# A planner's dates for the pieces of the turning groups, and three expert tiles as column pieces in the last group

## The chip, the core and the metric

The kernel runs on one core of one Trainium2 chip. The metric is the device time of one launch in microseconds, the median of several runs. The core's engines are TensorE (PE, with its weight loads as PEld), VectorE (DVE), ScalarE (ACT), GpSimd (POOL) and SyncE (SP); each works through its own instructions in program order, and they wait for each other by semaphores. DMAs are issued from the queues of SP and POOL.

## What is computed

The reference is one transformer layer on x of 4 x 2048 x 512 float32: xn = layernorm(x), and then x + attention(xn) + experts(xn).

```
qkv = xn @ w_qkv                          # 16 heads of 32
q, k = spectral_filter(q), spectral_filter(k)   # linear: folded into the weights
out = softmax(q k^T / sqrt(32)) v ; out @ w_out + b_out
# top-1 experts: one shared weight, capacity 100 for each of 8 experts
best = argmax(softmax(xn @ w_gate)); rank within the expert; tokens of rank >= 100 are dropped
y[token] = gate * (xn[token] @ w_expert + b_expert)   # at most 800 tokens
```

## The kernel before, in words

The work is a loop over 16 groups, numbered k = 0 to 15: 4 batches of 4 groups of 4 heads. A group is 4 blocks of 512 queries, a block 16 halves, a half one tile of 128 keys; so a group has 64 halves (GH) and the whole loop 1024. "Half 31 of group 7" is half 7 x 64 + 31. Two halves make a window. Nearly all instructions go through the helper `InOrder`, so that the profile gives them one line, 82, and one reads by the tiles' names.

A half has on PE: the scores of 4 heads against one tile of keys (`steps_of_keys,q`), the same for the row maxima of a block 21 halves ahead (`keys,q`), and the products of the half before with the values (`even,v`, `odd,v`, each over 32 columns for each head). DVE reduces the maxima (`part`) and adds up the products (`num`), ACT takes the exponentials into the tiles `even` and `odd` (3 buffers for odd), POOL issues a DMA for each window that adds odd to even, and adds windows on its own.

Beside that, each half executes a list of further steps, `agenda[half]`, in the order in which `at(half, step, cost=...)` (line 930) filled it. Costs are in pieces. A **piece** (cost 1) is one 128 x 128 tile of the next group's queries, keys or values, made by `query_key` or `value` from 32 matmul records of 128*32 weights by 128 columns, and copied out of PSUM by ACT; there are 48 for each group. Others are the closing of the block before (`fold` of the row sums in half 5 of a block, 8 reciprocals in halves 6 to 13, then, a block later, the output `result` in halves 1 to 4, cost 1 each, and the output's DMA `add` in half 5), the loads of weights by SP, and every fourth group the stage of the next batch. The four banks of PSUM beside the scores go round by age; a half with costs reduces two maxima together where their banks are neighbours (`max_reduce`).

In the **turning groups** k = 3, 7 and 11 the next batch's tokens are normalized (ACT) and turned (4 transposes on PE, an ACT copy, cost 0.5), and then routed to the experts by 29 steps (`plan_route`: gate scores, cost 4, transposes of the logits, exponentials, ranks and 16 entries into tables).

Who places the pieces: `plan(k)` is called for every group. In most groups it files the pieces in three queues (queries, keys, values) with a release and a last half each, and `level` gives each half, up to a load, the piece with the earliest last half, and looks ahead where it would rather wait. In the turning groups `spread` takes turns and pieces in one fixed order, written out by `projections`, and spaces them evenly by cost until the group's last half.

The experts (`expert_steps`, `place_experts`) come when all tokens are routed: from half 36 of group 12 on, 7 tiles of 128 slots are gathered from x by POOL's indirect DMAs, measured and scaled. `expert(i)` works as a pipeline: tile i is normalized, tile i - 1 turned, tile i - 2 multiplied by the expert weight in 4 full matmuls of 128 x 128 by 512 (cost 4), given its bias by DVE and its gate by ACT; the products fall into halves 2, 4 to 14 of group 13. Then each tile's rows of the output are gathered (POOL, `yg`), added (POOL) and scattered back, two halves apart, one tile in each block from group 13 on (halves 26, 42, 58 of group 13, 10, 26, 42, 58 of group 14). The gathers and scatters wait for the output's earlier DMAs.

The last group projects nothing further, so many of its halves have nothing on their agenda.

Of the kernel before, what the change touches and what calls it, by code (L numbers as in the profile page):

```python
# [12 lines left out]
F32 = mybir.dt.float32  # L13
# [21 lines left out]
ST = -(-SLOTS // P)  # L35
NTAB = 4
# [7 lines left out]
CROWDED = (1, (B - 1) * NG + 2)  # L44
# [57 lines left out]
def attention_and_top1_experts(ctx: ExitStack, tc: tile.TileContext, a: dict, out: bass.AP):  # L102
# [364 lines left out]
    def projections(k, tiles=1, kinds=None):  # L467
# [3 lines left out]
        if k == 0:  # L471
            order = [(query_key, 0, 1), (query_key, 0, 0)]
            order += [(query_key, n, 1) for n in range(1, NQ)] + [(query_key, 1, 0)]
            order += [(value, n) for n in range(NQ)] + [(query_key, n, 0) for n in range(2, NQ)]
        else:
            first = 2 if k in CROWDED else 3 if k % NG == 0 else 4
            queries, vals = ([(f, n, *s) for n in range(NQ)] for f, *s in ((query_key, 0), (value,)))
            news = [(query_key, n, 1) for n in range(NQ)]
            if first == 4:
                order = vals + queries[:2] + news + queries[2:]  # L480
            else:
                order = vals[:first] + queries[:1] + news[:3]
                order += vals[first : first + 1] + news[3:] + vals[first + 1 :] + queries[1:]
# [83 lines left out]
    def expert_steps():  # L567


        def begin():  # L570
# [15 lines left out]
            for half in xg:  # L586
                on.gpsimd.memset(half, 0.0)
# [3 lines left out]
            taken.update(mv=mv, w_exp=w_exp, b_exp=b_exp, entry=entry, index=index, bound=bound, xg=xg)  # L591

# [19 lines left out]

        def expert(i):

            if i >= 2:
# [11 lines left out]
            if 1 <= i <= ST:  # L627
                px = bank()
                for r in range(NR):
                    on.tensor.transpose(px[:, r * P : (r + 1) * P], row(i - 1)[:, r * P : (r + 1) * P], ident)  # L630
                taken["xt"] = work.tile([P, QB], F32, tag="byx", name="xt", bufs=1)
                on.scalar.copy(taken["xt"], px)
            if i >= 2:
                on.scalar.activation(row(i - 2), row(i - 2), AF.Copy, scale=taken["entry"][:, at, 1])
# [6 lines left out]
        return begin, fetch, measure, scale, expert  # L641

    def gather_row(i):
        taken["sum"] = work.tile([P, DM], F32, tag="byx", name="yg", bufs=1)
# [282 lines left out]
    heads = [[] for _ in agenda]  # L927
    costs = [0.0] * len(agenda)
    ended = {}

    def at(half, step, *args, cost=0):
        agenda[half].append(lambda: step(*args))
        costs[half] += cost
# [51 lines left out]
    def spread(steps, last, latest={}):  # L985


        base = steps[0][1]

        def places(level):  # L990
            half, done, found = base, costs[base], []
            for place, (cost, first, _) in enumerate(steps):
                stop = latest.get(place, last + 1)
                while half < stop and (half < first or done + cost / 2 > level * (half - base + 1)):
                    half += 1
                    if half > last:
                        return None
                    done += costs[half]
                done += cost
                found.append(half)  # L1000
            return found

        found = next(filter(None, (places(level / 32) for level in range(16, 400))))
        for (cost, _, step), half in zip(steps, found):
            at(half, step, cost=cost)
        return found

# [11 lines left out]
    def plan_route(first, step):  # L1019
# [3 lines left out]
        for i in range(ROUTE):  # L1023
            at(first + halves[i], step, i, cost=costs_of.get(i, 0))

    def place_experts(start):


        begin, fetch, measure, scale, expert = expert_steps()
        first = start + 36  # L1030
        at(first, begin)
        for i in range(ST):
# [3 lines left out]
        for i in range(ST + 2):  # L1036
            at(first + 26 + 2 * i, expert, i, cost=(NR if i >= 2 else 0) + (1 if 1 <= i <= ST else 0))
        for i in range(ST):
            free = start + GH + i * HB + 26
# [4 lines left out]
    def plan(k):  # L1044
# [3 lines left out]

        def after_keys_are_spent():

            for i, place in enumerate([j for j, s in enumerate(kinds) if s == 1]):
                cost, _, step = steps[place]
                steps[place] = cost, start + SPENT + i // TQ * TQ, step
                latest[place] = start + SPENT + i // TQ * TQ + 3 * TQ - 1

# [6 lines left out]
        last = start + GH - 1  # L1062
        steps, kinds, latest = [], [], {}
        if k == 0:
# [7 lines left out]
            plan_route(24, lambda i: first_route[i]())  # L1072
        if c == NG - 2 and b + 1 < B:
# [13 lines left out]
        if c < NG - 1 or k >= FREE:  # L1087
            for s in range(3):
                mine = [piece for piece, kind in zip(pieces, kinds) if kind == s]
                for i, piece in enumerate(mine):  # L1090
                    n = i // TQ
                    if s == 0:
                        stop = start + GH - MAX_AHEAD // 2 - 1 + n * HB
                        release = start + 1 + n * HB
                    elif s == 1:
                        release = start + SPENT + n * TQ
                        stop = release + 3 * TQ - 2
                    else:
# [226 lines left out]
```

## Time and profile before

| what | us |
|---|---|
| median of 3 runs | 4136.39 (4134.75 to 4137.25) |
| the profiled execution | 4136.57 |
| its span, first to last instruction | 4134.8 |
| PE busy | 4114.6 |
| DVE, POOL, ACT busy | 3416.0, 3016.6, 2487.0 |

The profile is of one execution. Its span leaves out 1.77 us around the instructions. PE's granted clock is full (1.00) throughout. "Busy" for matmuls includes the time for which they are in flight, and four matmuls over 32 columns each run at once; so a share of 100% says that PE always has something in flight, not how much work a stretch holds. For that one cuts the span into stretches and compares their lengths: the profile gives, for each stretch, its length and each engine's busy time with its count of instructions.

### The profile page before, as it was taken

To read this page: it belongs to the slowest core of one execution; us is meant where nothing else is said; L and a number is where in the kernel's file an instruction comes from. 1 tells how busy PE (TensorE), PEld (TensorE's weight loads), DVE (VectorE), ACT (ScalarE), POOL (GpSimd) and SP (SyncE) were. 2 spreads that over 40 slices of the span, in tenths; PEclk is the share of its full clock that TensorE was granted. 3 is DMA by queue.
4 is the path that set the end of the run, shared out by engine and by line. 5 is a ranking of instruction groups with operands and counts; after the bars stand their busy time and mean duration, and the time that the engine had idled before them with its cause. 6 is when DMAs were issued, how large, how long until landed. Compare 5 with 4: busy or idle time off the path is not lost.

```text
span 4134.8 us, 121347 instructions
## 1 busy us (share of the span) xinstructions
PE 4114.6 (100%) x52824; PEld 1834.2 (44%) x52824; DVE 3416.0 (83%) x4890; ACT 2487.0 (60%) x3424; POOL 3016.6 (73%) x2122
## 2 busy tenths in 40 slices
PE   8999999999999999999999999999999999999999
PEld 5444444444444444444444444444444444444433
DVE  7788887977888888897788888888778887888885
ACT  4555565676665556567565556566656555666665
POOL 1678776676887777676778777767678785787877
PEclk9999999999999999999999999999999999999999
DMA  4687887987788778898777887889877886788787
GB/s 127 144 164 155 162 163 158 227 189 144 153 158 162 156 158 167 189 208 187 143 152 157 162 162 154 169 192 205 171 154 153 174 164 132 162 166 171 158 163 154
DMA packets 179486, 680.78 MB, mean 165 GB/s; under 512 B 23478, under 2 KB 54360, under 8 KB 114184
## 3 DMA queue, kind: packets, MB, share of 16 engines
q0 software_dynamic: 109856, 601.63, 74.4%
q1 hardware_dynamic: 69024, 71.34, 5.2%
q8 instruction: 414, 6.78, 0.6%
q14 instruction: 120, 0.98, 0.1%
q10 hardware_dynamic: 72, 0.03, 0.0%
HBM read 71.07 MB, written 87.91 MB: 38 GB/s over the span
## 4 chain that ended last, share of the span: by engine, by line
PE 97%; DVE 2%; issue 0%; ACT 0%; DMA 0%; SPq 0%; ACTq 0%
PE array L82 97%; DVE part L82 2%; DVE num L82 0%; DVE factor L82 0%; DMA odd<-in_L_attn_w_qkv_dram 0%; ACT xs L82 0%; ACT xnT L82 0%; ACT odd L82 0%; DVE stats L82 0%; DVE xs L82 0%; ACT w L82 0%; DVE mv L82 0%; DVE neg L82 0%; SPq L82 0%; SPq L133 0%
## 5 line engine op out<-in xcount | busy, mean ns | idle before, releaser
L82 DVE TENSOR_REDUCE part<-array 128x1 f32<-128x512 f32 (+1 forms) x3089 | 2480.2, 858 | 641.1 <-PE array L82 636.1
L82 POOL TENSOR_TENSOR even<-even 128x1024 f32<-128x1024 f32 x876 | 2125.1, 2531 | 451.1 <-DMA even<-odd 450.3
L82 PE MATMUL array<-keys,q 32*128 32x512 f32 x8192 | 2049.2, 613 | 4.3 <-ACT keys L82 0.8
L82 PE MATMUL array<-q,steps_of_keys 32*128 32x512 f32 x8128 | 2015.1, 614 | 0.1
L82 ACT ACTIVATE odd<-array 128x1024 f32<-128x1024 f32 x1024 | 995.7, 1021 | 459.4 <-PE array L82 385.6
L82 ACT ACTIVATE even<-array 128x1024 f32<-128x1024 f32 x1014 | 983.8, 1021 | 420.7 <-PE array L82 412.6
L82 PEld LDWEIGHTS array<-keys,q 32*128 32x128 f32 x8192 | 767.2, 184 | 555.4 <-DVE part L82 341.0
L82 PEld LDWEIGHTS array<-q,steps_of_keys 32*128 32x128 f32 x8128 | 691.3, 184 | 242.3 <-issue 228.8
L82 DVE TENSOR_TENSOR num<-num,array 128x512 f32<-128x512 f32 x960 | 649.1, 676 | 32.8 <-PE array L82 31.3
L82 POOL DMA_DIRECT2D even<-odd x504 | 461.5, 916 | 278.8 <-ACT odd L82 237.0
L82 PEld LDWEIGHTS array<-xnT,w 128*32 128x32 f32 x16384 | 459.6, 110 | 276.9 <-DVE part L82 188.8
L82 PE MATMUL array<-odd,v 128*32 128x512 f32 x4096 | 545.7, 605 | 0.5 <-DVE part L82 0.5
L82 PE MATMUL array<-even,v 128*32 128x512 f32 x4056 | 540.4, 605 | 0.3 <-DVE part L82 0.3
L82 PE MATMUL array<-xnT,w 128*32 128x128 f32 x16384 | 531.8, 273 | 1.5 <-ACT xnT L82 1.0
L82 PEld LDWEIGHTS array<-w,xnT 128*32 128x32 f32 x8192 | 231.1, 110 | 145.6 <-DVE part L82 102.7
L82 DVE RECIPROCAL factor<-den 128x64 f32<-128x64 f32 x504 | 273.6, 544 | 0.0
L82 PE MATMUL array<-w,xnT 128*32 128x128 f32 x8192 | 269.8, 273 | 0.2
L82 PE MATMUL array<-wo,ot 128*32 128x512 f32 x2048 | 266.1, 592 | 0.0
L82 PEld LDWEIGHTS array<-odd,v 128*32 128x32 f32 x4096 | 81.0, 108 | 388.1 <-DVE part L82 380.3
L82 PEld LDWEIGHTS array<-even,v 128*32 128x32 f32 x4056 | 80.1, 108 | 384.5 <-DVE part L82 380.0
L82 POOL DMA_DIRECT2D out_dram<-y x63 | 85.6, 1359 | 164.1 <-ACT y L82 115.3
L82 ACT COPY q<-array 128x128 f32<-128x128 f32 x256 | 67.9, 265 | 178.4 <-PE array L82 178.4
(150 smaller groups left out, 1532.8 us busy)
## 6 DMA issues: line engine op xcount, KB each, us to landing
even<-odd POOLq DMA_DIRECT2D x504, 1024.0 KB, 8.2
out_dram<-y POOLq DMA_DIRECT2D x63, 1024.0 KB, 9.6
xs<-in_L_attn_x_dram SPq DMA_DIRECT2D x96, 256.0 KB
out_dram<-in_L_attn_x_dram SPq DMA_DIRECT2D x16, 1024.0 KB
w<-wd SPq DMA_DIRECT2D x30, 256.0 KB
w<-in_L_attn_w_qkv_dram SPq DMA_DIRECT2D x16, 256.0 KB
wo<-in_L_attn_w_out_dram SPq DMA_DIRECT2D x16, 256.0 KB
negm<-row SPq DMA_DIRECT2D x192, 4.0 KB
```

Of the source, the lines that this page charges most:

```text
L82: done = act(*args, **kwargs)
```

## The change

Four edits.

1. Turning groups file their pieces in the three queues like all others; `spread` is gone, and so is the special order of `projections`. Turns stand at dates written out by hand (`TURNS`, the halves in which `spread` had put them). A piece is released one half after the turn of the tile with its number. `level` then decides.
2. Normalizing, turns and the routing steps go into `tails`, which are appended to the agenda after `level`: they stand behind the pieces of their half.
3. Expert tiles 0 to 3 stay as they are. Tiles 4, 5 and 6 are turned in halves 14, 24 and 29 of the last group, and each is multiplied in four column pieces of 128 output columns (the same 32 matmul records as a value piece), with the bias added by DVE from PSUM, in halves 15, 16, 22, 23; 25 to 28; and 30, 31, 32, 38. Their gathers, adds and scatters follow in halves 25, 27, 29; 30, 32, 34; and 39, 41, 43 of the last group, and use the keys' weight buffer for the gathered rows.
4. The second memset of the gathered rows moves from half 36 to half 41 of group 12.

```diff
+EARLY = 4
+LATE = ((14, 15, 16, 22, 23), (24, 25, 26, 27, 28), (29, 30, 31, 32, 38))
...
-            first = 2 if k in CROWDED else 3 if k % NG == 0 else 4
...
+            order = [(query_key, n, s) for s in range(2) for n in range(NQ)] + [(value, n) for n in range(NQ)]
...
+        def turn_row(i):
+            px = bank()
+            for r in range(NR):
+                on.tensor.transpose(px[:, r * P : (r + 1) * P], row(i)[:, r * P : (r + 1) * P], ident)
+            taken["xt"] = work.tile([P, QB], F32, tag="byx", name="xt", bufs=1)
+            on.scalar.copy(taken["xt"], px)
+
+        def expert_columns(i, q):
+            cols = slice(q * P, (q + 1) * P)
+            pe = bank()[:, cols]
+            for r in range(NR):
+                columns(
+                    pe,
+                    taken["xt"][:, r * P : (r + 1) * P],
+                    taken["w_exp"][:, r, cols],
+                    start=(r == 0),
+                    stop=(r == NR - 1),
+                )
+            on.vector.tensor_tensor(row(i)[:, cols], pe, taken["b_exp"][:, cols], ALU.add)
+            if q == NR - 1:
+                on.scalar.activation(row(i), row(i), AF.Copy, scale=taken["entry"][:, i : i + 1, 1])
...
         def expert(i):
-            if i >= 2:
+            if 2 <= i < EARLY + 2:
...
     def gather_row(i):
-        taken["sum"] = work.tile([P, DM], F32, tag="byx", name="yg", bufs=1)
+        if i < EARLY:
+            taken["sum"] = work.tile([P, DM], F32, tag="byx", name="yg", bufs=1)
+        else:
+            taken["sum"] = weights.tile([P, NR, P], F32, name="w1", bufs=1).rearrange("p r n -> p (r n)")
...
+    def behind(half, step, *args, cost=0):
+        tails[half].append(lambda: step(*args))
         costs[half] += cost
...
         for i in range(ROUTE):
-            at(first + halves[i], step, i, cost=costs_of.get(i, 0))
+            behind(first + halves[i], step, i, cost=costs_of.get(i, 0))
...
+        at(first + 5, clear_rest)
...
+        tail = start + 3 * GH
+        for i, (turned, *places) in enumerate(LATE):
+            at(tail + turned, turn_row, EARLY + i, cost=0.5)
+            for q, half in enumerate(places):
+                at(tail + half, expert_columns, EARLY + i, q, cost=1)
         for i in range(ST):
-            free = start + GH + i * HB + 26
+            free = start + GH + i * HB + 26 if i < EARLY else tail + (25, 30, 39)[i - EARLY]
...
+            for i in range(NT):
+                turned[i] = start + TURNS[i]
+                behind(turned[i] - 1, in_stage, 3, i)
+                behind(turned[i], in_stage, 4, i, cost=0.5)
...
+                release = max(release, turned.get(i, start - 1) + 1)
...
+    TURNS = (2, 4, 6, 6, 6, 7, 7, 8, 12, 12, 12, 13, 16, 19, 21, 22)
...
     level(0, END)
+    for steps, last_ones in zip(agenda, tails):
+        steps += last_ones
```

## The prediction, on record before the changed kernel ran

> **What bounds the kernel now.** I read the page first, then the table by stretches, cut at the start of each half's value products (scores and maxima of half h+1 thus count in half h), then the chain of waits and POOL's timeline in the last group. TensorE is the bound nearly everywhere:
>
> ```profile
> PE 4114.6 (100%) x52824; PEld 1834.2 (44%) x52824; DVE 3416.0 (83%) x4890; ACT 2487.0 (60%) x3424; POOL 3016.6 (73%) x2122
> ...
> PE 97%; DVE 2%; issue 0%; ACT 0%; DMA 0%; SPq 0%; ACTq 0%
> ```
>
> Busy time does not tell how much a half costs; its length by what the planner put into it does. Six halves of group k = 7, numbers 8, 14, 16, 28, 29 and 31; the first columns are start:end, length and PE busy with its count:
>
> ```profile
> 1895.13:1899.65 4.52, 4.52 (x63) 2.11 (x60) 3.05 (x5) 2.70 (x5) 0.00 (x0) 1.00 0.98 224
> 1920.98:1924.78 3.80, 3.80 (x60) 1.79 (x56) 3.01 (x5) 2.21 (x4) 3.80 (x3) 1.00 0.94 188
> 1928.70:1933.08 4.38, 4.38 (x64) 2.21 (x60) 3.03 (x5) 2.81 (x5) 4.09 (x2) 1.00 0.90 181
> ...
> 1981.36:1986.04 4.68, 4.68 (x93) 2.64 (x89) 3.48 (x6) 2.49 (x5) 4.62 (x5) 1.00 0.63 130
> 1986.04:1989.46 3.42, 3.32 (x28) 1.14 (x24) 3.42 (x7) 2.25 (x3) 1.91 (x2) 1.00 0.91 208
> ...
> 1992.85:1998.51 5.66, 5.66 (x128) 3.62 (x125) 2.81 (x6) 2.76 (x7) 5.02 (x5) 1.00 0.87 177
> ```
>
> A piece is 32 matmul records. So a half without a piece (x28) takes 3.4 us, with one (x60) 3.80, with two (x93) 4.67, with three (x128) 5.66: the first costs 0.4, each further one 0.87. The empty half is not PE's: DVE is busy for all of its 3.42 us. The same lengths return in every group to about 0.02 us (a half with a result instead of a piece: 3.78, with both: 4.66; the last half of a block with one piece and with two: 3.91 and 4.79). So the sum can be made half by half, once it is known where the planner puts things; I worked its rules through for both versions, and for the one before they give the count of matmuls in each half of the trace.
>
> An expert tile beside the scores is dear (group 13, halves 12 and 14, the latter without a turn):
>
> ```profile
> 3451.28:3458.69 7.41, 7.41 (x41) 3.28 (x37) 4.59 (x7) 3.25 (x5) 5.90 (x5) 1.00 0.71 143
> ...
> 3462.49:3469.04 6.55, 6.55 (x36) 2.41 (x32) 3.70 (x6) 2.42 (x4) 5.43 (x3) 1.00 0.78 159
> ```
>
> In the last group, where halves 15, 16, 22 to 32 and 38 to 41 are empty, the chain of waits shows the cycle of such a half, which runs through DVE (reductions, sum, reciprocal) and not through PE:
>
> ```profile
> 3992.32 1.27 DVE part L82 x2
> 3993.59 0.59 DVE num L82
> 3994.19 0.46 DVE factor L82
> 3994.65 0.79 DVE part L82 x2
> ```
>
> **The change, part by part**, against the profiled execution (4136.57 us; span 4134.8 and 1.77 around it; 0.18 above the median of 4136.39).
>
> *Pieces in turning groups (k = 3, 7, 11).* The planner takes a piece out of nine halves: 24 (7.23 to 6.36, the length of half 24 of group 0, which has the gate scores and no piece), 28, 42, 56, 62 (4.67 to 3.80), 31 (5.66 to 4.79), 37 and 52 (4.66 to 3.78), 47 (4.79 to 3.91): 6 x 0.87 + 3 x 0.88 = 7.86. It fills 29 (3.42), 30 (3.39) and half 0 of the next group (3.44) to 3.80: 0.38 + 0.41 + 0.36; and doubles 32: 0.87. Net -5.84, three times: **-17.5**. The pieces do not vanish. After k = 3 and 7 five more fall into groups 6 and 10: halves 13, 14, 15, 16, 20, 21 go from one load to two (3 x 0.87 + 3 x 0.88 = 5.25), half 12 from two to one (-0.87): +4.38, twice: **+8.8**. After k = 11 three land in halves that the experts leave (next part), one in half 44 of group 14 (**+0.87**), one in the last group (below).
>
> *Expert tiles out of group 13.* Halves 10 and 12 go from 7.40 to 3.80 and half 14 from 6.56 to 3.80, each with one piece; half 8 keeps a tile and loses a turn of 4 transposes (34.1 us for 224: 0.61). 3.60 + 3.60 + 2.76 + 0.61: **-10.6**.
>
> *Columns in the last group.* A column piece has the 32 matmuls and shapes of a value piece, so each half goes to the length with a piece: 15 (3.43 to 3.91), 16 (3.41), 22 (3.43), 23 (3.39), 25 (3.39), 26 (3.64), 28 (3.42), 30 (3.39), 32 (3.42), 38 (3.43) to 3.80, 27 (3.60 to 4.00), 31 (3.27 to 3.91): +4.80. Turns: half 14 from 3.80 to 4.52; half 24 gets a turn and the piece left over, 3.39 to 4.52; half 29 a turn alone, 3.39 to 3.65 (half 0 of group 13): 0.72 + 1.13 + 0.26. Together **+6.9**.
>
> *Order.* Turns and routing steps now stand behind the pieces of their half. Of the halves shown, 8 (turn, then piece) took 4.52 and 16 (piece, then turn) 4.38; 13 and 22 are like 8. Three halves in three groups: 9 x 0.14 = 1.3. Group 0 has its routing steps ahead of the pieces, the turning groups already behind; the transposes of logits (half 26 of groups 0 and 7):
>
> ```profile
> 193.38:198.47 5.09, 5.04 (x65) 2.42 (x61) 4.29 (x8) 2.26 (x4) 3.42 (x2) 1.00 0.83 169
> ...
> 1972.89:1977.37 4.48, 4.45 (x65) 2.21 (x61) 3.84 (x8) 2.21 (x4) 3.43 (x2) 1.00 0.92 187
> ```
>
> That is 0.60; half 46 (4.64 against 4.44) and half 31 (4.94 against 4.79) give 0.35. Together **-2.2**. The Trainium skill, TensorEngine Tiling (Array Packing), Tiling Modes, says that a change of tiling mode, not of tile, drains the TensorE; a turn uses the full array between column tiles, so by that rule either order has two drains and this term would be 0. The rows speak against it.
>
> *DVE's share of a column piece.* A value piece is emptied by ACT (0.27), a column piece by DVE: 128x128 from PSUM, nearest row 0.29 (placed). In seven of the twelve halves (22, 23, 25 to 28, 38) a reciprocal stands ahead of it, and DVE has about 0.33 idle in a half with a piece and a reciprocal before the next reductions (timeline around 3935): nothing, if the add fits. Against that, the 0.22 of the block's negated maximum lengthens such a half from 3.80 to 4.00, and a measurement of 0.84 one to 4.10. Bounds 0 and 7 x 0.3 = 2.1; I take the nearest size, 7 x 0.2: **+1.4**. The bank is freed later too; that is in the 0.2.
>
> *POOL.* Three gathers (1.09), adds (1.59) and scatters (1.08) move to the last group: 11.3 us. Queued behind them on POOL are the pairs' DMAs, which free the odd buffers that ACT writes. From half 39 on:
>
> ```profile
> 4050.44 0.85 POOL L82 DMA_DIRECT2D even<-odd  x1
> 4056.40 4.67 POOL L82 TENSOR_TENSOR even<-even 128x1024 f32<-128x1024 f32 x2 [5.11 <-DMA even<-odd]
> 4061.03 0.73 POOL L82 TENSOR_TENSOR xnT<-keys 64x256 f32<-64x256 f32 x1
> 4061.72 0.84 POOL L82 DMA_DIRECT2D even<-odd  x1
> ...
> 4068.49 0.88 POOL L82 DMA_DIRECT2D even<-odd  x1
> ...
> 4070.30 1.22 POOL L82 DMA_DIRECT2D even<-odd  x1
> ```
>
> Tiles 4 and 5 meet 2.19, 2.03, 1.03 and 0.72 of idle time. The last gather (half 39) waits for the output DMA of 4040.44 (median 9.6 to landing) and fits into the 5.11. The last add and scatter (halves 41, 43), 2.7, meet a POOL without idle time until 4081.7. The pair of 4068.49 then lands later by 8.2 counted from its issue, at 4076.7, and ACT's odd tile started at 4076.89. Lower bound 0 (half 38 makes PE 0.4 to 0.6 later, and POOL may catch up); upper bound 5.0 (2.7, 1.25 left over from the scatter of half 34 with its issue, and the gather's 1.09 if its wait outlasts the 5.11). PE reads that tile's banks about 1.2 after ACT is done. I take 2.7 + 1.25 - 0.6 - 1.2, about **+2.0**. The memset moved to half 41 of group 12 (2.1) goes into POOL time before tile 4's fetch and costs nothing; if it were late, that fetch has five halves. The weight loads on SP go with the last piece of their kind, as before, and come at least five halves (19 us) ahead of the next pieces of that kind: 0; were one late, the first piece of its kind would wait for what is left of it.
>
> Sum: -17.5 + 8.8 + 0.9 - 10.6 + 6.9 - 2.2 = -13.7; + 1.4 + 2.0 = -10.3: **4126.3 us**.
>
> **Rivals.**
> *Both covers hold*: DVE's adds fit the 0.33 and POOL's lag is caught up. -13.7, 4122.9. For it: POOL idles 17 us from 3985 to 4061. Chance 0.22.
> *POOL decides the end*: both bounds, 2.1 + 5.0: 4136.57 - 13.7 + 7.1 = 4130.0. For it: no idle after 4056.4. Chance 0.17.
> *Order gives nothing* (what counts is the switch, not its neighbour; by the rule named above): 4126.3 + 2.2 = 4128.5. Against it: the rows of halves 16 and 26. Chance 0.11.
> *Slower: waits for the output on POOL's queue.* Gathers and scatters wait for each other and for the output's DMAs. At full price: 11.3 of work, 9.6 before the last gather, 3.5 (median landing) ahead of each add and of the second gather, 14: 34.9. Three odd buffers cover 4 halves, 15.2, less 0.9 and 8.2: 6.1. The rest, 28.8, would stall PE: 4136.57 - 13.7 + 1.4 + 28.8 = 4153. It makes the kernel slower from 13.7 - 1.4 + 8.3 = 20.6 uncovered. Against it: between gather and add lie two halves, and POOL's idle time. Chance 0.05.
>
> **Numbers.** Forecast 0.45, own range 4124.3 to 4128.3. A measurement of this kernel tells 0.2% (8.3 us, so 4128.1) from no change. Faster: the first rival, 0.40 of the forecast and 0.03 of the third, 0.65. Same: the second, the rest of the third and 0.05 of the forecast, 0.30. Slower 0.05. Range 4122.0 to 4130.5: from the first rival, less a little, to just past the second.
>
> **What would show it.** Halves 29 and 30 of groups 3, 7, 11 at 3.80 with x60, half 31 at x93; half 13 to 16 of groups 6 and 10 at 4.67; no 7.4 in group 13 after half 8; halves 22 to 28 of the last group at 3.8 (adds fit) or 4.0; ACT odd waiting for a DMA near half 49 (POOL). Wrong, if an empty half costs more than 3.80 once it has a column piece, or if the doubled halves of groups 6 and 10 lose more than 0.87.

## The result, and the profile after

| what | us |
|---|---|
| kernel before, median of 22 runs | 4136.64 (4134.75 to 4138.56) |
| changed kernel, median of 22 runs | 4131.34 (4129.44 to 4133.74) |
| ratio | 0.9988, 95% interval 0.9982 to 0.9993 |
| profiled execution of the changed kernel, and its span | 4130.40, 4128.6 |

The change saves 5.3 us, 0.12%, where 10.3 were forecast; 4131.3 lies above the range. Between the profiled executions the difference is 6.17, of which 1.24 come from the stretch ahead of the loop, which the change does not touch; so the halves give 4.93, and these are what has to be explained. The profiled execution of the changed kernel is 0.94 below its median. One half may account for that: half 32 of group 4 takes 4.67 in it, as in the kernel before, but 5.3 to 6.3 in 15 of the 18 profiles of kernels with the turning edit (this one and those of the experiments). With the turning edit alone, PE stands still there for 1.19 us inside a piece, and the profile names nothing that it waits for.

From the page of the changed kernel, its busy times and the chain that ended last, in which DMA has 1% (0% before) and POOL now appears:

```profile
PE 4105.5 (99%) x53184; PEld 1832.0 (44%) x53184; DVE 3418.3 (83%) x4876; ACT 2486.1 (60%) x3424; POOL 3015.6 (73%) x2122
...
PE 97%; DVE 1%; DMA 1%; POOL 0%; issue 0%; ACT 0%; SPq 0%; POOLq 0%; ACTq 0%; DVEq 0%
```

PE's busy time fell by 9.1 us, the span by 6.2. So PE is idle for 2.9 us more than before, and the chain says that some of its waiting is for DMAs.

The table by stretches again, cut at the same places (start:end, length, PE busy with its count; the third column from the end is the granted clock). Half 26 of group 0; halves 8, 29 and 31 of group 7; half 13 of group 6; half 12 of group 13; halves 22 and 23 of the last group:

```profile
192.14:196.62 4.48, 4.45 (x64) 2.20 (x60) 3.84 (x8) 2.22 (x4) 3.42 (x2) 1.00 0.94 190
1890.75:1895.14 4.39, 4.39 (x64) 2.22 (x61) 3.06 (x5) 2.71 (x5) 1.75 (x2) 1.00 1.14 261
...
1979.50:1983.30 3.80, 3.80 (x60) 1.79 (x56) 3.48 (x6) 2.20 (x4) 3.21 (x2) 1.00 0.99 226
...
1987.10:1991.89 4.79, 4.79 (x97) 2.71 (x93) 3.00 (x5) 2.72 (x6) 4.44 (x4) 1.00 0.82 166
1651.95:1656.62 4.67, 4.67 (x92) 2.63 (x89) 3.48 (x6) 2.74 (x5) 4.07 (x3) 1.00 0.97 176
...
3436.71:3440.51 3.80, 3.80 (x61) 1.79 (x57) 3.48 (x6) 2.22 (x4) 3.74 (x5) 1.00 0.60 121
...
3970.16:3974.13 3.97, 3.97 (x61) 1.93 (x57) 3.79 (x7) 2.12 (x3) 3.43 (x2) 1.00 1.15 214
3974.13:3977.93 3.80, 3.80 (x60) 1.88 (x57) 3.45 (x7) 2.27 (x4) 0.86 (x1) 1.00 1.06 220
```

All of these are as forecast, to about 0.02 us where one length was named: an empty half filled to 3.80, a triple one down to 4.79, a doubled one at 4.67, the expert's half at 3.80. For halves 22 and 23 two lengths were named, 3.8 and 4.0, and each has one of them. The time that is missing sits in four other halves: half 36 of group 12, and halves 46, 49 and 50 of the last group. In the kernel before (half 46 took 2.51 there) they read:

```profile
3278.13:3282.09 3.96, 3.96 (x36) 1.28 (x32) 3.96 (x9) 2.12 (x3) 3.36 (x3) 1.00 1.11 200
...
4078.00:4080.92 2.92, 2.92 (x26) 0.73 (x25) 0.69 (x1) 2.54 (x3) 2.92 (x3) 1.00 1.09 246
4080.92:4083.84 2.92, 2.92 (x28) 0.73 (x24) 1.38 (x2) 1.39 (x2) 0.76 (x1) 1.00 0.97 272
```

and in the changed kernel, with half 46:

```profile
3264.94:3272.03 7.09, 4.03 (x37) 1.28 (x33) 3.90 (x9) 3.30 (x4) 6.40 (x5) 1.00 1.03 191
...
4057.57:4060.64 3.07, 3.03 (x18) 0.75 (x16) 0.69 (x1) 2.68 (x3) 2.67 (x6) 1.00 0.28 64
4066.88:4073.33 6.45, 4.14 (x26) 1.01 (x25) 0.69 (x1) 3.29 (x4) 6.45 (x4) 0.96 1.03 239
4073.33:4077.65 4.32, 4.32 (x26) 0.91 (x24) 1.38 (x2) 2.10 (x3) 0.24 (x1) 0.67 1.03 263
```

They cost 3.13, 0.56, 3.53 and 1.40: 8.6 us. Half 36 is idle for 3.06 and half 49 for 2.31 (length less PE busy). Half 50 is different: PE is busy for all of it with the usual 26 records, and the clock column says 0.67. It is not waiting but slow.

Two chains of waits say what was late. First around half 36 (start, duration, what), then around half 49:

```profile
3258.19 2.36 POOL even L83
...
3260.72 2.17 DMA table<-entry,slot
...
3262.90 7.88 DMA entries<-table
...
3270.97 0.31 DVE entry L83 x2
```

```profile
4047.81 2.35 POOL even L83
...
4052.04 5.54 POOL even L83 x3
...
4057.74 1.08 POOL out_dram L83
...
4060.39 9.54 DMA even<-odd
...
4070.04 1.03 ACT odd L83
```

In half 36 of group 12 the expert stage begins: VectorE reduces the table entries, which SyncE loads after POOL's last routing scatter. That scatter stands behind POOL's additions of pairs, and went out 8.2 us after the start of its half 33, where it took 4.85 before. In the kernel before, the load was issued at 3272.77 and VectorE came to the entries at 3280.89 without a wait:

```profile
3280.89 0.30 DVE L82 TENSOR_REDUCE entry<-entries 128x7 f32<-128x28 f32 x2
```

With the 7.88 of the load shown here that left some 0.2 us of room. Now POOL is 3.3 us later against PE, and VectorE waits 3.19.

POOL became late in the shortened turning group. Taking the issue of each pair's DMA (a pair is the even and the odd tile of a window) less the start of its half: in group 11 both kernels agree up to half 36; the changed kernel is 0.9 us later in half 56, 2.1 in half 58, 2.7 at the start of group 12, and 3.3 in half 34 there. PE was given less to do, POOL and its DMAs were not.

What carries the lateness along is the DMAs more than POOL's own instructions. In halves 6, 22 and 38 of group 12 both kernels issue the pair at the same distance from the start of the half, so POOL has caught up there. But the pair of half 6 lands 15.5 us after its issue in place of 13.1; POOL waits for it with nothing else to do in both kernels (4.3 and 4.6 us), adds it later in the changed one, and is late again. The last 0.8 of the 3.3 appear at half 32 of group 12, which takes 5.39 in the profile of the kernel before and 4.67 in this one; so part of the wait in half 36 is time that PE had gained there. Two other profiles fit that (without tile 6's rows, and with the order turned back: half 32 is 0.36 and 0.45 longer, half 36 is 0.39 and 0.41 shorter), the one with the turning edit alone does not.

In the last group tile 6's scatter (4057.74) and the addition before it stand between the pairs; the DMA that frees ScalarE's odd buffer goes out 8.09 us after the start of half 44 (4.51 before) and lands 9.54 later (8.29 before).

### The profile page after: what moved, and what is told of

Its sections match the earlier page's. It is cut to its first block, busy times and chain, and to the rows that moved or that the text cites. A ratio compares the mean times of both kernels' runs of the same rounds, so it can differ in the third digit from the quotient of the medians.

```text
span 4128.6 us, 122052 instructions
## 1 busy us (share of the span) xinstructions
PE 4105.5 (99%) x53184; PEld 1832.0 (44%) x53184; DVE 3418.3 (83%) x4876; ACT 2486.1 (60%) x3424; POOL 3015.6 (73%) x2122
## 3 DMA queue, kind: packets, MB, share of 16 engines
q8 instruction: 416, 6.82, 0.6%
## 4 chain that ended last, share of the span: by engine, by line
PE 97%; DVE 1%; DMA 1%; POOL 0%; issue 0%; ACT 0%; SPq 0%; POOLq 0%; ACTq 0%; DVEq 0%
PE array L83 97%; DVE part L83 1%; POOL even L83 0%; DMA even<-odd 0%; DMA entries<-table 0%; DMA odd<-in_L_attn_w_qkv_dram 0%; ACT xs L83 0%; DVE num L83 0%; ACT xnT L83 0%; DVE factor L83 0%; DMA table<-entry,slot 0%; DVE stats L83 0%; POOL out_dram L83 0%; ACT odd L83 0%; POOL rest L83 0%
## 5 line engine op out<-in xcount | busy, mean ns | idle before, releaser
L83 ACT COPY keys<-array 128x128 f32<-128x128 f32 x256 | 68.2, 266 | 176.8 <-PE array L83 172.3
```

Of the source, the lines that this page charges most:

```text
L83: done = act(*args, **kwargs)
```

## The experiments

My theory after this comparison: the two edits work as calculated, and two waits that hang on POOL's lateness take 8.6 us back. ("The begin" is the step that begins the expert stage in half 36 of group 12.) Rivals: the stall at the begin comes from the moved memset or the experts' edit; the begin of the stage costs this much anywhere; what is short at the end is the DMA queue's bytes and not POOL. Each run is given with its ratio to the kernel before on the same chip (95% interval); on two of the five chips the kernel before itself took 4140 us, and there only ratios and lengths of halves are compared.

**One edit without the other.** First the turning groups and the order alone, with all tiles in group 13 as before; then the late tiles alone.

> The turning groups' edit and the tails alone; all seven expert tiles as in the kernel before. Three pieces go to halves 28 of groups 13 and 14 and to halves 15, 16, 22 of the last group. Theory 'POOL late': the stall at half 36 of group 12 is there (7.1 against 3.96), as it comes from the turning groups; groups 0 to 12 as in the changed kernel (-8.9), +0.87 twice and +1.24: about 4130.7. Rival 'experts' edit makes the stall' (moved memset): half 36 at 3.96 and 4127.6.

Measured: 4132.67, ratio 0.9989 (0.9979 to 0.9998). Half 36 stays at 7.08, halves 46, 49 and 50 are back at 2.51, 2.93 and 2.92. The stall is there without the late tiles. The memset stays moved in this run, so it alone does not clear the memset. Something else was new, halves 36 and 37:

```profile
3266.50:3273.58 7.08, 4.03 (x36) 1.28 (x32) 3.90 (x9) 3.30 (x4) 6.21 (x4) 1.00 1.07 198
3273.58:3279.03 5.45, 5.45 (x32) 1.48 (x33) 3.14 (x5) 1.20 (x2) 2.68 (x2) 0.69 1.02 170
```

After the idle 3.05 us the next half ran at a clock of 0.69 and took 1.67 longer. In the changed kernel's profile the same idle time was followed by 1.00 and 3.78.

> The three late expert tiles alone (and the moved memset), turning groups as in the kernel before. Theory 'POOL late': half 36 of group 12 stays at 3.96. Group 13 falls by 10.6 to 10.8; in the last group columns and turns give +5.6, the pieces that leave halves 12 to 14 about -1.0, DVE's adds +1.3, and by theory 'rows on POOL' the end +5.4: sum about +0.5, 4137. So this edit alone brings nothing. Rivals: half 36 at 7 and 4140; or no stall at the end without the other edit, and 4131.7.

Measured: 4137.21, ratio 1.0002 (0.9993 to 1.0012). Group 13 gives 10.81, the last group takes 12.81, and half 36 of group 12 has 0.62 of waiting, where none was expected. The memset is moved here too, and the stall of 3.1 is not there: it takes the turning edit. The moved memset, which now stands five halves behind the stall, is out. Alone this edit brings nothing.

**The begin of the expert stage, two halves later.**

```diff
-        at(first, begin)
+        at(first + 2, begin)
...
-            at(first + 2 + 2 * i, fetch, i)
+            at(first + 4 + 2 * i, fetch, i)
```

> The changed kernel with the experts' begin step (loads of the tables, DVE's two reductions of the entries) and its seven gathers two halves later, begin in half 38 of group 12. Theory 'POOL late': the faster turning group leaves POOL 2 to 3 us further behind PE, the last table entry lands late and DVE stands still for 3.2 us at begin; two halves (7.6 us) later the entries are there. Half 36 falls from 7.09 to about 3.9, half 38 stays at 3.8 to 4.1, the total falls by 3.1 against the changed kernel: about 4128.2. Rival 'begin itself' (its weight loads or the memset that was moved cost the time): the stall moves to half 38 and the total stays at 4131.3.

Measured: 4130.88, ratio 0.9986 (0.9976 to 0.9995), near the 4131.3 of the rival and not the 4128.2 of the theory. Half 36 is back at 3.96, as the theory has it, but half 38 goes from 3.80 to 5.74. Not for the load: VectorE did not wait for the entries. Its timeline in half 38, beside POOL's (start, duration, engine, operation):

```profile
3277.05 4.67 POOL L83 TENSOR_TENSOR even<-even 128x1024 f32<-128x1024 f32 x2 [3.98 <-DMA even<-odd]
3277.11 2.31 DVE L83 CAST who<-entry 128x7 int32<-128x7 f32 x1
```

The conversion of 7 numbers per partition takes 0.17 in the kernel before and in the changed one. Here it starts 0.06 after POOL's additions and ends at 3279.42, 0.03 after the first of the two. Two runs test that:

> The kernel with the beginning of the expert stage in half 38 (fetches two halves later), with one thing changed: the conversion of the row numbers to integers is done by ScalarE in place of VectorE. Theory (VectorE's conversion waits for POOL's addition beside it: 2.31 us from 3277.11 to 3279.42, while POOL's additions began at 3277.05): half 38 falls from 5.74 to 3.80 - 4.0 us, ScalarE's copy takes 0.2 to 0.3 us, and the time is 1.7 to 1.9 us under that of the kernel with VectorE's conversion, about 4129.0 us. Rival (half 38 is long from the load of the entries or from the reductions): half 38 stays at 5.5 to 5.8 us and the time at 4130.9 us.

Measured: 4130.19, ratio 0.9983 (0.9973 to 0.9992). The conversion takes 0.20 on ScalarE, and half 38 takes 4.26, 1.48 less than with VectorE's conversion; 0.46 of the 1.94 stay, and why is not shown. (Halves 44 to 51 of this profile are 1.5 us longer than the changed kernel's, and the time misses the expected 4129.0.)

> The changed kernel with the expert stage's beginning (loads, VectorE's reductions of the table entries, conversion of the row numbers) one half later, in half 37 of group 12; the fetches of rows stay where they were. Theory (VectorE waits 3.19 us in half 36 for a load of table entries that POOL's late scatter holds back, and in half 38 the conversion of the row numbers took 2.31 us in place of 0.17 us because POOL's 128x1024 addition of a softmax pair ran at the same time): in half 37 POOL waits for the pair's DMA, so the entries are there and the conversion keeps its 0.17 us; half 36 falls from 7.09 to 3.96, halves 37 and 38 keep their lengths within 0.2, and the time is 4131.3 - 3.1 = 4128.2 us. Rival (the beginning costs some 2 us wherever it stands): half 37 or 38 grows by about 1.9 us, and the time is about 4130.2 us. Rival (the load itself is late by more than a half): 0.5 to 2 us stay as a wait of VectorE for the entries.

Measured: 4129.81, ratio 0.9983 (0.9973 to 0.9992). Half 37 takes 3.78, half 38 3.80, and half 36 is back at the length that it had before:

```profile
3266.00:3269.96 3.96, 3.96 (x37) 1.28 (x33) 3.79 (x6) 2.12 (x3) 3.05 (x3) 1.00 0.97 169
```

Every other half of the loop is that of the changed kernel to 0.11, but for one with 0.32. The whole stall is gone for a shift by one half, into a place where POOL is not adding: it runs a memset, beside which the conversion takes 0.71, and half 37 is no longer for it. By the halves the theory holds, and "it costs 2 us wherever it stands" falls; the time alone, between the 4128.2 of the one and the 4130.2 of the other, would not tell them apart.

**The rows of the late tiles.** First tile 6's gather, addition and scatter left out.

> The changed kernel without the gather, add and scatter of tile 6 (halves 39, 41, 43 of the last group); the last tile's expert rows are thus missing in the output, its matmuls stay. Theory 'rows on POOL': they delay the pairs' DMAs by some 3.6 us, and with them the odd buffers that ACT needs in halves 47 to 51: halves 46, 49 and 50 go from 3.07, 6.45 and 4.32 back to about 2.5, 2.9 and 2.9, the total falls by about 5.4 to 4125.9. Rival 'columns' (it is the column pieces and their later banks that put the last block out of step): no change, 4131.3.

Measured: 4127.51, ratio 0.9977 (0.9968 to 0.9987), where 4125.9 was expected. Halves 46, 49 and 50 are back at 2.51, 2.92 and 2.93; half 51 has 1.42 of waiting instead, so 4.07 are gained and not 5.4. It is these rows. Can they be put elsewhere? All three tiles' rows into halves 24 to 34:

```diff
+ROWS = ((24, 26, 27), (26, 29, 30), (30, 33, 34))
```

> The changed kernel with the gathers, additions and scatters of the three late tiles in halves 24 to 34 of the last group (tile 4: 24, 26, 27; tile 5: 26, 29, 30; tile 6: 30, 33, 34) in place of halves 25 to 43, and the column pieces in halves 23 to 32; the planner then puts one projection piece into half 45 of group 14 instead of half 24 of the last group. Theory (POOL is behind by 4.7 to 8.1 us in halves 44 and 46 because tile 6's row work stands in halves 39 to 43): POOL has caught up before half 44, halves 46, 49 and 50 are 2.5, 2.9 and 2.9 us long again, and the time is 4131.3 - 5.4 = 4125.9 us, to 4127.3 if 1.4 us stay in a half behind as without tile 6's rows. Rival (the three tiles' rows make POOL late wherever they stand): halves 30 to 36 grow by 3 to 5 us where ScalarE waits for the pair's DMA, and the time is 4129 to 4131 us.

Measured: 4138.54, ratio 1.0003 (0.9993 to 1.0012): the rival's mechanism, in later halves and dearer than it said. Halves 49 and 50 are 2.93 each, but halves 37, 43 and 44 take 2.3, 2.4 and 3.2 more (half 44 at a clock of 0.54); the wait came sooner and grew. With the begin in half 37 beside it:

> The two moves together: rows of the late tiles in halves 24 to 34 of the last group, and the beginning of the expert stage in half 37 of group 12. Theory: the two gains add up, 4131.3 - 5.4 - 3.1 = 4122.8 us, which is the time that the prediction gave for the case in which both covers hold (4122.9). Rivals: only the rows' move holds, 4125.9; only the beginning's, 4128.2; the gain of one is taken back by an idle stretch of TensorE in another place, 4126 to 4130.

Measured: 4134.76, ratio 0.9995 (0.9985 to 1.0004), far from the 4122.8 of the theory. Half 36 gains its 3.13, halves 37 and 43 to 45 lose 9.0 and 49 and 50 gain 4.9.

Then tile 6 alone, gathered in 34, added in 39, scattered in 41:

> The kernel with the beginning of the expert stage in half 37 (4129.81 us), with tile 6's rows moved further from the end of the last group: gathered in half 34, added in 39, scattered in 41, in place of 39, 41 and 43. Nothing else is moved. Theory (POOL comes late to the last pairs because in half 39 it waits 1.58 us for the store of y ahead of tile 6's gather, and issues gather and scatter, 1.1 us each, between the pairs): the pair DMA that was issued at 4060.39 goes out about 2.7 us sooner, ScalarE's wait of 4.27 us in half 49 falls to about 1.5, halves 46, 49 and 50 lose 2.5 to 3.5 of their 5.4 us, and the time is 4129.8 - 2.7 = 4127.1 us. Rival (what is short is the DMA queue, busy 86 % in halves 36 to 46, and not POOL's place in the order: moved rows only delay an earlier pair): halves 46, 49 and 50 lose less than 1 us, or as much is lost in halves 35 to 44, and the time is 4129.5 to 4130.5 us.

Measured: 4137.01, ratio 0.9991 (0.9982 to 1.0). Halves 49 and 50 are 2.93 and 2.92, but 44 takes 4.06, and 46, 47 and 48 take 3.2, 2.8 and 1.6 more at clocks of 0.75, 0.50 and 0.50. POOL's additions wait 3.10 for a pair that was issued at 4037.14, right behind the 1 MB store of y, and landed only 15.5 us later. Moving the rows does not help.

**What is short, bytes or POOL's time?** Four runs on one chip; the first is the kernel with the begin in half 37, as the reference.

> The kernel with the beginning of the expert stage in half 37, unchanged, as the reference for the other three on the same chip: half 46 about 3.0, 49 about 6.5 and 50 about 4.2 us, halves 44 to 51 (the eight) about 29.2 us together, and a time of 4129 to 4131 us; on a chip whose DMAs are slower, 3 to 5 us more, as for the kernel before (4140.2 in place of 4136.6).

Measured: 4133.97, ratio 0.9985 (0.9976 to 0.9995), halves 44 to 51 26.66 us together, 2.5 less than expected. Halves 49 and 50 of this run:

```profile
4070.83:4077.03 6.20, 3.90 (x27) 1.02 (x25) 0.69 (x1) 3.05 (x4) 6.20 (x4) 1.00 1.05 243
4077.03:4079.95 2.92, 2.92 (x26) 0.72 (x24) 1.38 (x2) 1.40 (x3) 0.53 (x1) 1.00 1.08 295
```

PE's idle time is 2.30, as in the changed kernel, but the clock stays at 1.00, and half 50 costs nothing. So, taking this run as the one without the clock, of the 5.5 us at the end of the changed kernel's profile 0.25 and 1.40 are the clock, and 3.28 and 0.56 the wait.

> The kernel with the beginning in half 37, with tile 6's rows gathered and scattered for the first 256 of the 512 columns only, and its addition done in two halves of 256 columns so that GpSimd's work stays (tile 6's expert product is missing from the other half of the columns of the output). If the DMA queue is short: 256 KB less at some 200 GB/s, 1.3 us, and halves 44 to 51 lose 1.0 to 2.5 us. If GpSimd's time is short: gather, scatter and additions still take 1.1, 1.1 and 1.3 to 1.5 us of it, and the sum of halves 44 to 51 stays within 0.5.

Measured: 4133.54, ratio 0.9983 (0.9974 to 0.9993), no faster in its halves (44 to 51: 29.80; of the 3.1 more than in the reference, 0.94 and 2.13 are halves 49 and 50 at clocks of 0.83 and 0.56). The pair goes out 8.18 us after the start of half 44 (8.14 in the reference), and ScalarE waits as before:

```profile
4075.09 1.94 ACT L83 ACTIVATE odd<-array 128x1024 f32<-128x1024 f32 x2 [4.25 <-DMA even<-odd]
```

ScalarE starts 9.6 us after the issue in both runs. 256 KB less buy nothing, and the theory of the bytes falls. The sum of the halves met neither expectation, because of the clock. The number of rows is unchanged in this run, so whether the DMA queue is short by transfers and not by bytes is not tested.

> The kernel with the beginning in half 37, with the additions of the three late tiles' rows done by VectorE in place of GpSimd (halves 27, 32 and 41 of the last group). If GpSimd's time is short: 1.3 to 1.6 us less for it per tile, the pair of half 48 goes out at least 1.3 us sooner, halves 46, 49 and 50 lose 1.3 to 3 us together, against up to 3 x 0.7 that VectorE adds in halves 27, 32 and 41 (0.3 each, if its idle time there takes half of it): 0.5 to 2 us faster than the reference. If the DMA queue is short: halves 44 to 51 keep their sum within 0.5, VectorE's 0.3 to 2.1 us are added, and the time is 0 to 2 us above the reference.

Measured: 4137.72, ratio 0.9992 (0.9982 to 1.0002). Halves 44 to 51 fall to 23.51, but half 32 takes 8.84 (5.04 more), 33 2.41 and 41 2.31 more. VectorE's and POOL's timeline in half 32:

```profile
4015.26 4.86 POOL L83 TENSOR_TENSOR even<-even 128x1024 f32<-128x1024 f32 x2
...
4016.31 5.04 DVE L83 TENSOR_TENSOR xg<-xg,w 128x512 f32<-128x512 f32 x1 [0.68 <-DMA w<-out_dram,who]
...
4019.86 0.93 POOL L83 TENSOR_TENSOR xnT<-keys 64x256 f32<-64x256 f32 x1
```

VectorE's additions of this size with one operand in PSUM take 0.68 on the mean, also beside POOL. This one has both operands in SBUF, starts during POOL's additions and ends at 4021.35, 0.56 after the last of POOL's three (4020.79). The same addition took 0.68 in half 27 and 2.39 in half 41. So the run is no clean test of POOL's time: the end is relieved because PE came 10 us later.

> The kernel with the beginning in half 37, two late tiles in place of three, and their rows' additions on VectorE. With two late tiles halves 44 to 51 were 1.7 us shorter on another chip; by the terms (group 13 +3.5, group 14 +0.9, the last group -2.3 and -2 to -4 at its end) it is 0 to 2 us faster than the reference; if GpSimd's time is short, VectorE's additions take another 0 to 1.3 us off, if the DMA queue is short, they add 0.3 to 1.4. Rival: what is left at the end with two late tiles is neither, and the additions show only in halves 27 and 32.

Measured: 4137.79, ratio 0.9995 (0.9985 to 1.0005). Halves 44 to 51 take 23.10, but 32 and 33 take 4.4 and 1.6 more than with POOL's additions: in half 32 the addition waits 2.12 for its gathered rows and then takes 2.76. The expected gain of 0 to 2 us is missed for this reason, and again PE came later to the end.

> The kernel with the beginning in half 37 and three late tiles, with tile 6's addition left out, so that its rows of the output get the expert product alone without x and attention; gather and scatter stay. If GpSimd's time between the pairs counts: the pair's DMA of half 48 goes out 1.26 us sooner (8.1 us after the start of half 44 becomes 6.8), half 49 falls from 6.2 - 6.5 to about 5.0, half 50 by 0 to 1.3, and halves 44 to 51 from 26.7 - 28.2 to 25.4 - 26.5 us. If it is the scatter ahead of the pair in the DMA queue alone: the pair still lands 9.5 us after its issue, and the sum of halves 44 to 51 stays within the 1.5 us by which two runs of this kernel differ.

Measured: 4127.52, ratio 0.9978 (0.9969 to 0.9987). The pair goes out at 6.96 instead of 8.01 (the kernel with the begin in half 37), 1.05 sooner, but its DMA takes 10.02 instead of 9.51, so it lands 0.54 sooner; half 46 is 2.51 again and half 49 stays at 6.56. Half of the gain of POOL's time was lost to the DMA's length, and the expected 5.0 for half 49 was missed. Neither reading is confirmed alone.

**How many late tiles?** With the begin in half 37 in all: two late tiles, one, none. The run with one leaves tile 5's product out (the pipeline of group 13 ends a step earlier), which shortens group 13 by some 2.8 to 3.6 us; so only its last group is compared.

> The kernel with the beginning of the expert stage in half 37 (4129.81 us), with two late tiles in place of three: tile 4's product stays whole in group 13 as before, tiles 5 and 6 take the column dates of the first two (turns 14 and 24, pieces in 15 to 28, rows in 25 to 34). By the terms: group 13 +3.5 (a third of 10.6), a second projection piece in half 45 of group 14 +0.9, the last group -2.3 (four column pieces and a turn) and -4.0 in halves 46, 49, 50 and 51 (as measured without tile 6's rows): 4129.8 - 1.9 = 4127.9 us. Rival (two tiles' rows in halves 25 to 34 make POOL late by themselves, as in the kernel with all rows sooner): 2 us or more appear in halves 37, 43 or 44, and the time is 4130 to 4132 us.

> The kernel with the beginning in half 37, with tile 6 alone as column pieces (turn in half 14, pieces in 15, 16, 22, 23, rows in 25, 27, 29 of the last group). If row work near the end is what eats the gain: with the rows done by half 29, halves 44 to 51 are back at 22.8 to 23.5 us as in the kernel before (26.4 with two late tiles, 28.2 with three); against two late tiles group 13 gains a tile (+3.5), group 14 loses its two doubled halves (-1.7), the last group four pieces and a turn (-2.3) and 2.5 to 3.6 at its end: 8 to 11 us below the kernel before. Rival: the end of the last group keeps 1.5 us or more of wait, because TensorE is faster there than GpSimd whatever the rows do: 6 to 8 us below the kernel before.

> The turning groups' edit and the order alone, with all seven expert tiles in group 13 as before, and the beginning of the expert stage in half 37. By the measured group sums without the stall of 3.1 us: groups 3, 7, 11 and the halves after them -18.7, groups 6 and 10 +8.7, group 0 -1.0, groups 13 to 15 +0.9 to +2: 8 to 9 us below the kernel before, so that the late experts would add nothing to it or take from it. Rival: half 37 keeps the 1.7 us by which it was longer with the turning edit alone, or the beginning's wait moves into it: 5 to 7 us below.

| late tiles | time | ratio | pair issued after the start of half 44 | halves 44 to 51 |
|---|---|---|---|---|
| three | 4129.81 | 0.9983 (0.9973 to 0.9992) | 8.01 | 28.16 |
| two | 4133.32 (chip of 4140) | 0.9983 (0.9974 to 0.9992) | 8.09 | 26.42 |
| one (see above) | 4124.72 | 0.9970 (0.9958 to 0.9982) | 6.82 | 25.05 |
| none | 4128.34 | 0.9980 (0.9971 to 0.9989) | 4.13 | 22.79 |

One tile's rows in halves 25 to 29, fifteen halves away, already make the pair 2.7 us late: the rival of the run with one tile. POOL itself wins the time back. In half 38 it issues the pair as early as without late tiles (1.6 us ahead of the start of the half), and between halves 30 and 44 it stands idle for 9.5 us until pairs have landed, against 5.6 without late tiles. What stays late is the DMAs, as in group 12; why they do is not shown. Two late tiles did not give the 1.9 us that were expected of them (half 44 takes 1.25 more than with three, half 46 0.9); without any the expected 8 to 9 us below the kernel before came as 8.2. And three late tiles against none, summed over the halves: 11.7 us less in group 13, 12.1 more in the last group, of which 1.6 are the clock's. The late tiles bring nothing. The version without them has the lowest ratio of the complete ones and is faster than the kernel before; its interval overlaps that of the changed kernel and of the versions at 0.9983, so that it beats these is not shown. Beside the turning edit it needs one changed line.

**The order.** Turns and routing steps ahead of the pieces again, dates unchanged:

```diff
-        tails[half].append(lambda: step(*args))
+        agenda[half].append(lambda: step(*args))
```

> The changed kernel with the order of a half turned back: turns, pair sums and routing steps are issued ahead of the projection pieces of the same half, as in the kernel before; the dates stay. By the prediction's term for the order (-2.2 us: nine halves by 0.14 and 0.95 in group 0): halves 8, 13 and 22 of groups 2, 6 and 10 go from 4.38 back to 4.52, half 26 of group 0 from 4.48 to 5.08, half 31 from 4.79 to 4.94, half 46 from 4.44 to 4.64, the turns in halves 14 and 24 of the last group may each gain or lose 0.14, and the time is 4131.3 + 2.2 = 4133.5 us. By the rival (the order gives nothing: either order has as many changes of the array's form): these halves keep 4.38 and 4.48, and the time is 4131.3 us.

Measured: 4146.74, ratio 1.0015 (1.0006 to 1.0024), against 0.9988 for the changed kernel and far above the 2.2 us that were expected. The halves that were named went the way of the forecast, half 13 further: 8, 13 and 22 to 4.52, 4.65 and 4.52, half 26 of group 0 to 5.09, 31 to 4.99, 46 to 4.65. But so did others that I had not counted, since this run turns them back further than the kernel before had them: 16 to 4.66, 26 and 46 of the turning groups by 0.60 and 0.21, 11 and 12 by 0.15 together. That is 1.8 in each turning group and 1.0 in group 0: 6.4 us for the order alone, where I had set down 2.2. The rest of the distance between the ratios, some 5 us, is not settled: this profile has 1.64 more in half 37 of group 12, at a clock of 0.69 behind the wait at the begin, and single halves (16, 26, 27, 32, 59 of several groups) that are 0.2 to 0.9 longer, many of them also in the two other profiles taken on this chip, for a reason that the profiles do not name.

## Why the prediction was wrong

*Pieces in turning groups, doubled halves, half 44.* Right. With the order, the turning groups give 6.2, 6.2 and 6.2 with the half behind them (forecast 5.84 and three times 0.14: 6.26), groups 6 and 10 take 4.31 and 4.37 (4.38), group 14 0.87.

*Expert tiles out of group 13.* Right, 10.81 for 10.6: half 8 fell to 6.55, not to 6.8. A turn beside a tile costs 0.85, not the 0.61 that its 4 transposes came to by their mean time.

*Columns, turns and VectorE's share.* Right, 8.5 for 6.9 + 1.4. The additions cost 0.17 in halves 22, 25 and 38, 0.26 in 26, 0.57 in 27 and nothing in 23 and 28: 1.34.

*Order.* Right for the halves named, and the sign was tested: turning it round costs what the rows say. The rule of the Trainium skill that I weighed (TensorEngine Tiling (Array Packing), Tiling Modes) would have given nothing; these runs show 0.14 to 0.60 a half, and the measurement decides.

*"The memset moved ... costs nothing", weight loads 0.* Right in the profile: neither shows a wait.

*POOL, about +2.0.* **Wrong in size**: 5.5 in the profile. The lateness of the pair was about right: 2.7 + 1.25 - 0.6 = 3.35 forecast, 8.09 - 4.51 = 3.58 measured. But I let the DMA land after 8.2, and it took 9.54; with that and the slack of 1.2 the wait is 3.6, near the 3.84 measured. The rest, 1.65, is the clock that fell after PE's idle time, which no row of before could show, since PE never stood idle in its loop for more than 0.5 us. Why the DMA got longer stays open: not for the scatter's bytes (half of them gave the same wait), and not for the scatter alone, since it took 9.23 in the run with one late tile, which has none near. The second rival, POOL decides the end (+5.0), named the right place and had the better number; whether it is POOL's time or its DMAs that decide there, the runs do not settle.

*What was not in the sum at all.* **3.13 us in half 36 of group 12.** I priced each half by what the planner puts on PE, and asked POOL's question (what frees later?) only for the edit that gives POOL new work. The turning edit gives it none. But it takes 5.8 us from PE in each turning group, and what hung on POOL's DMAs with 0.2 us to spare was then late. So the step that failed is that the turning edit got a price on PE (-17.5, which came) and none on POOL's queue: that the last table entries would land later against PE and hold up the begin was put at nothing without a reason. The run with the begin moved by one half shows this wait and nothing else going away.

So the miss of 5.4 us in the halves is 3.1 from a step that was not priced and 3.5 from the end, less 0.7 in half 32 of group 12, whose length differs between 4.67 and 5.39 from profile to profile, and some tenths in the terms above. The other rivals fell: the covers did not hold, the order counts, and POOL's waits for the output stayed far from the 28.8 us of the slower one (1.58 ahead of the last gather).

## What to carry to other kernels

When an edit shortens the bounding engine's work in a stage, list what in that stage and the next hangs on the other engines with little room, as if those engines had become slower by the same amount. Count the DMAs that such an engine issues as an engine of their own: here POOL had idle time again soon, and its DMAs stayed late. Before moving work to an "empty" place, price it there for every queue that it enters, and look whether the lateness heals before the end; here three tiles moved gave 11.7 us and took 12.1. Where a wait is found, try the step one place further first.

## What the runs showed of the hardware

**VectorE behind POOL.** A conversion of 128x7 took 2.31 us beside POOL's additions, in place of 0.17, and ended 0.03 after the first of them. In the eleven runs with the begin in half 37 it took 0.66 to 0.72 beside a memset of POOL's and ended 0.02 to 0.03 after it. On ScalarE it took 0.20 beside the same additions. An addition of 128x512 with both operands in SBUF took 0.68 where it began with POOL idle, and 5.04, 2.39 and 2.76 where it began during one of POOL's additions; these three ended 0.55 to 0.56 after the end of one of POOL's instructions. The Trainium skill, SBUF — State Buffer, in the section on SBUF's two separate sides, says that VectorE and GpSimd share a pair of ports as an exclusive lock, and that the loser waits for the whole instruction. The conversions agree, and the additions of 2.39 and 2.76, which waited for one instruction; the one of 5.04 let three of them pass.

**The clock after a short idle time.** PE idle for 2.2 to 3.1 us was followed by a granted clock of 0.5 to 0.7 for one half or more in some profiles (0.67 after 2.31, 0.69 after 3.05, 0.50 after 2.23), and by none in others (1.00 after 2.30 and after 3.06). So a wait of this size costs more than itself, or not, by chance: nothing or 1.4 to 1.7 us in the profiles shown, 3.1 in the run with half of the rows (clocks of 0.83 and 0.56 in halves 49 and 50), 4.4 in the run with tile 6's gather in half 34 (0.50 in halves 47 and 48). The Trainium skill, TensorE: Matmul & The Clock Gate, Part 1, has the clock halved after at least one idle window of about 3.4 us that runs freely. That the outcome differs fits a free-running window; the idle times seen here are shorter than 3.4 us.

**A pair behind a store.** The accumulating DMA of 1 MB took 8.3 us in the median of the changed kernel's 313 pairs with a landing in the profile, and 12.5 in the median of the 31 among them that were issued next behind a store of 1 MB (10.2 to 16.6).
